# The last batch of a cross-attention kernel: two sets of four PSUM banks in turn, the keys' third chunk projected inside the batch, and a third head's sum off VectorE

## The chip, the cores and the metric

The kernel runs on one core of one Trainium2 chip. The metric is the device time of one execution in microseconds (us). All data are float32. Before the change, four runs took 459.06, 458.02, 459.40 and 457.72 us: the median is 458.54 us. The profiled execution is the one of 459.06 us; its span, from the first to the last instruction on the core, is 457.3 us.

Names used below: PE is TensorE, DVE is VectorE, ACT is ScalarE, POOL is GpSimd, SP is SyncE, on whose queue nearly all DMAs are issued. L617 is line 617 of the kernel. PSUM, where PE writes, has eight banks here, each used as a tile of 128 x 512.

## The reference, cut to what matters

Eight batches; 112 query rows of 320 channels, 20 heads of 16 channels; 371 text rows and 4 prompt rows of 512 channels for each batch.

```python
q, k_t, v_t = heads(x @ W_q), heads(text @ W_k), heads(text @ W_v)
probs_t = softmax(q @ k_t.T * 16 ** -0.5)            # per head: 112 x 371
text_out = probs_t @ v_t
attn_scores = q @ heads(ip @ W_k_ip).T * 16 ** -0.5   # per head: 112 x 4
qsem = l2norm(probs_t @ text)                         # per head: 112 x 512
sem = qsem @ l2norm(ip).T
probs_ip = softmax(attn_scores + 0.5 * sem) * spatial_mask
ip_out = probs_ip @ heads(ip @ W_v_ip)
out = (text_out + ip_out) @ W_out + b_out + x
```

## The kernel before

**Groups.** The 20 heads of a batch are worked on in five groups of four (`groups`, L70): groups 0 and 1 take heads of the first 128 channels, 2 and 3 those of the second 128, group 4 those of the last 64 channels (the third chunk). The norm of `qsem` needs, for each head, p G p' with G the Gram matrix of the text rows; only its diagonal is needed. So for each head PE multiplies the transposed probabilities with a tile `u`, which holds the upper triangle of G with its diagonal halved, the products with the normalised prompts, a column of ones and the values of the head (`multiplied`, L603). That gives 392 columns for each head in one PSUM bank (`ps_qd`): the first 371 are summed against `p`, and the last 21 are copied out as `pvs`. The four heads of a group lie in four row strips of the array and run side by side; a group is 12 rounds j of four matmuls that get 32 columns narrower from round to round, each in two passes.

**The stages of a group**, each two groups ahead of the next: `scores` on PE (112 x 371 into a bank of its own); `probabilities`, which is the row maximum `nmx` on DVE (L582), the exponential `p` on ACT (L586) and a DMA of `p` into `xg` on SP's queue (L589); `transposed`, one large transpose `xgT` on DVE (L597); then `multiplied` on PE; then the copy of `pvs` (L630) on ACT and the sum `junk`, `ss` on DVE (`reduced`, L657). With LEAD = 2, the scores of group g+2 are issued among the rounds of group g, and DVE does the transpose of group g+1 right behind the four `nmx` of group g+2.

**Order.** PE, SP and DVE run in the order in which the code is written; ACT too in the main loop, and POOL too in the last batch. `p` has three buffers for each head group (L584, `bufs=3`), so that the exponential of group g+3 writes where `p` of group g was.

**The last batch** (b = 7, from L999) has no next batch whose projections could fill PE's waits. Four steps differ there. In groups 0 to 2 (`g <= LEAD`) the first two heads' sums are taken off DVE (`shared`, L632): ACT copies the product out of PSUM (L642), POOL multiplies it with `p` (L646), and ACT sums it (L650). The banks are chosen by hand: `ps_qd` has four banks, `ps_sc` (`bank(..., spare=True)`) two and `ps_mm` (`bank(...)`) two. The prompts' part of batch 6 is finished with a block-diagonal matrix `bd`: `own_channels` (L519) cuts `bd` out with a memset and two selections on POOL. And `finish` (L670) is stepped by hand: its parts stand between the groups' work on DVE, ACT, POOL and PE.

**The end of a batch**, `finish`: `z`, `rn` (DVE, from `pvs` and `ss`), square root (ACT, L704, which needs a load of its function table, and another one back to the exponential, L705), `zr` (L707) and `attn` (POOL, L710), `rn`, `fu`, `mx`, `fu` (DVE, L715 to L721), `ex` (ACT, L725), `sx`, `rx`, `w` (DVE, L729 to L733); then with `bd` the transpose `ps_wT` (PE, L739) and its copy (ACT, L743), the matmuls `ps_a` (PE, L749 and L752), their copy `aT` (ACT, L760), the output projection `ps_o` (PE, L767) and `ob` (DVE, L780), which goes out by DMA (L783). For batch 6 this runs among groups 2 to 4 of batch 7 and behind them. Batch 7 is finished in two parts: `first` (heads 0 to 15, with `bd`) and `last` (heads 16 to 19, without it).

**Two more helpers.** `keys` (L433) projects the keys in three chunks; for all batches but the first, the third chunk's 64 channels come out of `values` (L460), whose matmuls are 384 columns wide instead of 320, and are copied by POOL (L476) and transposed by PE (L441). `prompt_logits` (L542) multiplies the queries with the prompts' keys (`ps_ip`, three small matmuls) and copies the result on ACT (`ipl`, L556).

Of the kernel before, what the change touches and what calls it, by code (L numbers as in the profile page):

```python
# [8 lines left out]
F32 = mybir.dt.float32  # L9
AF = mybir.ActivationFunctionType  # L10
ALU = mybir.AluOpType
# [9 lines left out]
def kernel(  # L21
# [343 lines left out]

    def awake(n, end=False):

        if end:
            ps = ps_qd.tile([P, 512], F32, tag="qd", name=f"ps_w_{n}")
        else:  # L370
            ps = bank(f"ps_w_{n}", spare=True)
        for _ in range(n):
            nc.tensor.matmul(ps[:, :P], ident, ident, start=True, stop=True)  # L373

# [58 lines left out]
    def keys(b):  # L433
        s = st[b]
        for i in range(NC):
            ps = bank(f"ps_k_{b}_{i}")
            if b > 0 and i == FULL:

                for c in range(NT):
                    rows = min(P, TT - c * P)  # L440
                    nc.tensor.transpose(  # L441
                        ps[:, c * P : c * P + rows],
                        s["k3"][:rows, c].rearrange("p a r d -> p (a r d)"),
                        ident[:rows, :rows],
                    )
                nc.scalar.copy(s["kT"][:, i, :], ps[:, :TT])
                yield
                return
            for e in range(NE):
                nc.tensor.matmul(  # L450
                    ps[:, :TT],
                    wk_sb[:, e, i * P : (i + 1) * P],
                    s["ctxT"][:, e, :TT],
                    start=(e == 0),
                    stop=(e == NE - 1),
                )
            nc.scalar.copy(s["kT"][:, i, :], ps[:, :TT])  # L457
            yield

    def values(b):  # L460
        s = st[b]
        ctxT, vext = s["ctxT"], s["vext"]
        w = C + REST if b > 0 else C
        for c in range(NT):
            ps = bank(f"ps_v_{b}_{c}")
            for e in range(NE):
                nc.tensor.matmul(  # L467
                    ps[:, :w],
                    ctxT[:, e, c * P : (c + 1) * P],
                    wv_sb[:, e, :w],  # L470
                    start=(e == 0),
                    stop=(e == NE - 1),
                )
            nc.scalar.copy(vext[:, c, :w], ps[:, :w])  # L474
            if w > C and c == NT - 1:
                nc.gpsimd.tensor_copy(  # L476
                    s["k3"][:, :, :, 0, :],
                    vext[:, :, C:].rearrange("p c (a d) -> p c a d", d=D),
                )
            yield  # L480
# [122 lines left out]
    def multiplied(b, g):  # L603
        s = st[b]
        xT = s.pop(("xT", g))
        banks = []
        for a in range(GROUP):


            if b == B - 1 and (g, a // 2) in ((1, 0), (2, 1), (3, 1), (4, 1)):  # L610
                banks.append(bank(f"ps_qd_{b}_{g}_{a}", spare=g == 3))
            else:
                banks.append(ps_qd.tile([P, 512], F32, tag="qd", name=f"ps_qd_{b}_{g}_{a}"))
        for j in range(BLK):
            c, q = j // QN, j % QN
            for a in range(GROUP):
                nc.tensor.matmul(  # L617
                    banks[a][:S, j * RG : UW],
                    xT[a * RG : (a + 1) * RG, j, :S],
                    region(b, c)[a * RG : (a + 1) * RG, q, q * RG :],  # L620
                    start=(j == 0),
                    stop=(j == BLK - 1),
                )
            yield
        s["qd", g] = banks
# [6 lines left out]
    def shared(b, g):  # L632

        s = st[b]
        some = list(enumerate(zip(groups[g], s["qd", g])))[:2]
        t = work.tile([P, NE, TP], F32, tag="ctxT", name=f"shared_{b}_{g}")
        prods = [t[:S, a, :TT] for a, _ in some]
        p = s["p", g]
        for a, (h, ps) in some:
            if b == B - 1:  # L640
                nc.scalar.copy(s["pvs"][:, h, :], ps[:S, TT:UW])
            nc.scalar.copy(prods[a], ps[:S, :TT])  # L642
        yield

        for a, _ in some:
            nc.gpsimd.tensor_tensor(prods[a], prods[a], p[:, a, :], ALU.mult)  # L646
        yield

        for a, (h, _) in some:
            nc.scalar.activation(prods[a], prods[a], AF.Copy, accum_out=s["ss"][:, h : h + 1])  # L650
        yield
# [18 lines left out]
    def finish(b, heads=(0, H), eng=None, late=False, bd=None):  # L670
# [18 lines left out]
        if not late:  # L689
# [14 lines left out]
        nc.scalar.activation(rn, rn, AF.Sqrt)  # L704
        nc.scalar.preload_act_table(AF.Exp)  # L705
        zr = sm("zr")
        nc.vector.reciprocal(zr, z)  # L707
        attn = attn_ring[b % 2]
        ah = attn[:, :C].rearrange("p (h d) -> p h d", d=D)[:, part]
        eng.tensor_tensor(  # L710
            ah, pvs[:, :, NIP + 1 :], zr.unsqueeze(2).to_broadcast([S, n, D]), ALU.mult
        )
        yield

        nc.vector.reciprocal(rn, rn)  # L715
        fu = sm4("fu")
        nc.vector.tensor_tensor(fu, pvs[:, :, :NIP], over_ip(rn), ALU.mult)
# [13 lines left out]
        nc.vector.reciprocal(rx, sx)  # L731
        w = sm4("w")
        nc.vector.scalar_tensor_tensor(w, ex, sm_sb, over_ip(rx), ALU.mult, ALU.mult)  # L733
        yield

        i0, i1 = h0 * D // P, -(-h1 * D // P)
        if bd is not None:
            ps = ps_qd.tile([P, 512], F32, tag="qd", name=f"ps_wT_{b}")
            nc.tensor.transpose(  # L739
                ps[: n * NIP, :S], w.rearrange("s h n -> s (h n)"), ident[:S, :S]  # L740
            )
# [45 lines left out]
    def prompt_sums_and_projection(b, s, eng, part, n, h0, h1, i0, i1, w, attn, ah, late):  # L787
# [14 lines left out]
            eng.tensor_tensor(ah, ah, wv[:, 1], ALU.add)  # L802
        yield

        ps = bank(f"ps_a_{b}_{h0}", spare=True)
        for i in range(i0, i1):
            nc.tensor.transpose(
                ps[:, i * S : (i + 1) * S], attn[:, i * P : (i + 1) * P], ident[:S, :S]
# [34 lines left out]
    def between(b, g):  # L843
# [26 lines left out]
        if g == 3:  # L870
            if new:
                run(("k", nb), None, 1)
            for bs in first if b > 0 else ():
                run(("q", bs[0]), lambda: project_queries(bs), 3)
            if new:
                run(("t", b), lambda: prompt_logits(b))
            if new:
                run(("k", nb), None, 1)
            if b > 0 and new:
                run(("f", b - 1), None)  # L880
            for bs in rest:
                run(("q", bs[0]), None)
        if g == 4:
            if nb + 1 < B:
                run(("c", nb + 1), lambda: transposed_context(nb + 1))
            if b > 0 and new:
                run(("f", b - 1), None, 2)
            if nb + 1 < B:
                run(("c", nb + 1), None, 2)
            for bs in (first if b > 0 else []) + rest:  # L890
                run(("q", bs[0]), None)
            if nb == B - 1:
                run(("t", nb), lambda: prompt_logits(nb))

    prompts = normalised_prompts()
    context = transposed_context(0)
# [103 lines left out]
    b = B - 1  # L1000
    before = ("f", b - 1)

    places = {0: {0: (2, 3), 1: (0, 1)}, 1: {0: (2, 3), 2: (0, 1)}, 2: {0: (2, 3), 2: (0, 1)}}
    for g in range(NG):
        own = {}
        for a in (0, 1) if g in places else ():
            if g == 0:
                own[a] = bank(f"ps_s_{b}_{g + LEAD}_{a}")
            elif g == 2:
                own[a] = ps_qd.tile([P, 512], F32, tag="qd", name=f"ps_s_{b}_{g + LEAD}_{a}")  # L1010
        for j, _ in enumerate(multiplied(b, g)):
            for a in places.get(g, {}).get(j, ()):
                if g == 1 and a < 2:
                    own[a] = ps_qd.tile([P, 512], F32, tag="qd", name=f"ps_s_{b}_{g + LEAD}_{a}")
                scores(b, g + LEAD, a, ps=own.get(a))
                probabilities(b, g + LEAD, a)
            if j != 2:
                continue
            drain(sums)
            if g == 2:  # L1020
                run(before, lambda: finish(b - 1, bd=bd[:, 0]))
            if g + 1 < NG:
                transposed(b, g + 1)
            if g == 3:
                run(before, None, 2)
                nc.scalar.preload_act_table(AF.Sqrt)  # L1026
        if g <= LEAD:
            sums = shared(b, g)
            next(sums)
            value_sums(b, g, 2)  # L1030
            reduced(b, g, 2)
        else:
            value_sums(b, g)
            if g == NG - 1:
                run(before, None)
                next(first)
                run(before, None)
                nc.scalar.preload_act_table(AF.Sqrt)
                run(before, None)
            reduced(b, g)  # L1040
        if g + 1 < NG:
            placed(b, g + 1)
        if g <= LEAD:
            next(sums)
        if g == 0:
            run(("f", b - 2), None)
        if g == 1:
            prompt_values(b)
            own_channels(bd)
        if g == 2:  # L1050
            run(before, None)
        if g == 3:

            first = finish(b, (0, FULL * HC), bd=bd[:, 1])
            next(first)
            next(first)
            run(before, None)
            next(first)
# [58 lines left out]
```

## Time and profile before

| what | us |
|---|---|
| median of four runs | 458.54 (457.72 to 459.40) |
| the profiled run, and its span | 459.06, 457.3 |
| busy in the span: PE, DVE, ACT, POOL | 437.8, 308.8, 191.0, 107.8 |
| busy in the last 17 us: PE, DVE, ACT, POOL | 11.14, 6.08, 4.17, 0.00 |
| one transpose `xgT` (L597), one `nmx`, one `p`, one `junk` | 2.97, 0.53, 0.57, 0.54 |
| one POOL product of `shared` (L646), one selection on `bd` (L524) | 0.97, 1.00 |

A busy PE is not PE at its peak, since matmuls are pipelined. The chain of waits follows the work that ended last back from the last instruction; in this execution it goes back to 410.92 us, into the last batch. In a timeline row the numbers are start and length in us, then engine, line, operation, tiles and count, and in brackets how long the engine was idle before it and whom it waited for. In a table of stretches, each row gives the stretch, its length, and busy time (and instructions) of PE, of PE's weight loads, DVE, ACT and POOL, then PE's granted clock as a share of full speed, the share of DMA and its GB/s.

### The profile page before, as it was taken

What the parts mean: (1) busy time and instruction counts of PE and PEld (TensorE: products, weight loads), DVE (VectorE), ACT (ScalarE), POOL (GpSimd) and SP (SyncE); (2) the same over time, 40 slices, a digit from 0 to 9 for tenths busy, and PEclk for the clock granted to TensorE, in tenths of its full rate; (3) what the DMA queues carried; (4) which work ended last, traced back from release to release, by engine and by line L of the source; (5) the groups of instructions that cost most, each with busy time, mean ns of one, the idle gap of its engine ahead of it and who ended that gap; (6) DMA issues with size and microseconds to landing.
All of it is one profiled execution on the core that took longest, in us unless ns stands there. A gap on an engine that the chain in (4) does not pass through costs nothing. (4 is left out here: it accounts for less than half of the span.)

```text
span 457.3 us, 12952 instructions
## 1 busy us (share of the span) xinstructions
PE 437.8 (96%) x5132; PEld 340.0 (74%) x5132; DVE 308.8 (68%) x657; ACT 191.0 (42%) x531; POOL 107.8 (24%) x260
## 2 busy tenths in 40 slices
PE   8998999999999999999999999999999999988855
PEld 8756867877777877887778877887768777878743
DVE  3047466786677768786676668787677668778763
ACT  2254233345334353345334353345335353355631
POOL 4302200102051114212061113312050213336400
PEclk9999999999999999999999999999999999999967
DMA  8569954645646454645646554545655355535200
GB/s 251 154 172 258 200 158 109 148 129 162 160 127 163 141 135 137 146 131 165 170 115 155 156 147 130 138 139 154 170 139 137 118 131 157 140 88 156 58 0 25
DMA packets 52158, 64.83 MB, mean 142 GB/s; under 512 B 18370, under 2 KB 44146, under 8 KB 52098
## 3 DMA queue, kind: packets, MB, share of 16 engines
q1 hardware_dynamic: 51658, 63.45, 52.2%
q8 instruction: 40, 0.66, 0.6%
q10 hardware_dynamic: 440, 0.56, 0.4%
q14 instruction: 20, 0.16, 0.1%
HBM read 19.30 MB, written 5.32 MB: 54 GB/s over the span
## 5 line engine op out<-in xcount | busy, mean ns | idle before, releaser
L617 PE MATMUL ps_qd<-u,xgT 32*112 32x104 f32 (+11 forms) x3840 | 216.6, 351 | 5.5 <-DVE xgT L597 3.2
L617 PEld LDWEIGHTS ps_qd<-u,xgT 32*112 32x112 f32 x3840 | 183.8, 172 | 39.1 <-issue 9.1
L582 DVE TENSOR_REDUCE nmx<-ps_s 112x1 f32<-112x371 f32 x160 | 77.6, 529 | 75.0 <-PE ps_s L569 74.3
L597 DVE STREAM_TRANSPOSE xgT<-xg 128x1536 f32<-128x1536 f32 x40 | 118.9, 2972 | 7.5 <-DMA xg<-p 7.5
L586 ACT ACTIVATE p<-ps_s,nmx 112x371 f32<-112x371 f32 x160 | 82.5, 572 | 64.3 <-DVE nmx L582 52.3
L657 DVE CUSTOM_DVE_ANT_0 junk<-ps_qd,p 112x371 f32<-112x371 f32 x152 | 82.4, 542 | 18.1 <-ACT pvs L630 2.0
L538 POOL COPY u<-vr 128x64 f32<-128x64 f32 x120 | 26.2, 240 | 173.6 <-PE ps_qd L617 117.7
L467 PE MATMUL ps_v<-wv_sb,ctxT 128*128 128x384 f32 (+1 forms) x192 | 64.7, 487 | 0.0
L569 PE MATMUL ps_s<-kT,qm 32*112 32x371 f32 x320 | 63.8, 475 | 0.4 <-ACT p L586 0.4
L467 PEld LDWEIGHTS ps_v<-wv_sb,ctxT 128*128 128x128 f32 x192 | 35.2, 190 | 20.8
L450 PE MATMUL ps_k<-ctxT,wk_sb 128*128 128x371 f32 x136 | 45.9, 482 | 0.0
L630 ACT COPY pvs<-ps_qd 112x21 f32<-112x21 f32 x154 | 16.1, 190 | 64.9 <-PE ps_qd L617 64.8
L414 PE MATMUL ps_g<-ctxT 128*128 128x375 f32 (+2 forms) x168 | 37.4, 379 | 0.0
L450 PEld LDWEIGHTS ps_k<-ctxT,wk_sb 128*128 128x128 f32 x136 | 25.1, 190 | 15.4 <-issue 0.5
L414 PEld LDWEIGHTS ps_g<-ctxT 128*128 128x128 f32 x168 | 28.1, 190 | 8.4
L569 PEld LDWEIGHTS ps_s<-kT,qm 32*112 32x112 f32 x320 | 26.1, 171 | 4.8 <-ACT kT L457 2.1
L312 DVE TENSOR_SCALAR qm<-ps_q,emask 128x224 f32<-128x224 f32 (+1 forms) x25 | 9.2, 400 | 26.2 <-PE ps_q L303 26.1
L474 ACT COPY vext<-ps_v 128x384 f32<-128x384 f32 (+1 forms) x24 | 11.3, 472 | 27.2 <-PE ps_v L467 26.6
L457 ACT COPY kT<-ps_k 128x371 f32<-128x371 f32 x17 | 8.0, 469 | 26.8 <-PE ps_k L450 26.8
L402 ACT ACTIVATE ug<-ps_g 128x375 f32<-128x375 f32 (+2 forms) x24 | 9.0, 377 | 23.0 <-PE ps_g L414 19.8
L403 POOL TENSOR_TENSOR ug<-ug,half 128x128 f32<-128x128 f32 (+1 forms) x24 | 10.8, 452 | 29.6 <-ACT ug L402 29.6
L789 POOL TENSOR_TENSOR wv<-vip,w 112x1280 f32<-112x1280 f32 x6 | 14.8, 2462 | 11.3 <-DVE w L733 11.3
(123 smaller groups left out, 331.2 us busy)
## 6 DMA issues: line engine op xcount, KB each, us to landing
xg<-p SPq DMA_DIRECT2D x160, 162.3 KB
u<-ug SPq DMA_DIRECT2D x128, 99.0 KB
ct<-in_ctx_dram SPq DMA_DIRECT2D x16, 256.0 KB
vip<-vipd SPq DMA_DIRECT2D x7, 560.0 KB
vr<-vd SPq DMA_DIRECT2D x32, 120.0 KB
vd<-vext SPq DMA_DIRECT2D x7, 320.0 KB
ct<-in_ctx_dram SPq DMA_DIRECT2D x8, 224.0 KB
vd<-vext SPq DMA_DIRECT2D x7, 160.0 KB
```

What stands on the lines that cost most here:

```text
L414: nc.tensor.matmul(ps[:, : T - t0], ctxT[:, e, t0 : t0 + P], ctxT[:, e, t0:T], start=(e == 0), stop=(e == NE - 1),)
L450: nc.tensor.matmul(ps[:, :TT], wk_sb[:, e, i * P : (i + 1) * P], s["ctxT"][:, e, :TT], start=(e == 0), stop=(e == NE - 1),)
L467: nc.tensor.matmul(ps[:, :w], ctxT[:, e, c * P : (c + 1) * P], wv_sb[:, e, :w], start=(e == 0), stop=(e == NE - 1),)
L538: nc.gpsimd.tensor_copy(region(b, c)[:, :, UV - c * P :], s["vr"][:, c * QN : (c + 1) * QN, g, :])
L569: nc.tensor.matmul(ps[:S, :TT], qm[a * RG : (a + 1) * RG, i, r, j * S : (j + 1) * S], s["kT"][a * RG : (a + 1) * RG, i, :], start=True, st ...
L582: nc.vector.tensor_reduce(nmx, ps[:S, :TT], AX.X, ALU.max, negate=True)
L586: nc.scalar.activation(p, ps[:S, :TT], AF.Exp, bias=nmx)
L597: nc.vector.transpose(xT.rearrange("p j (k q) -> p q j k", q=QN), xg.rearrange("p q (j k) -> p q j k", k=RG),)
L617: nc.tensor.matmul(banks[a][:S, j * RG : UW], xT[a * RG : (a + 1) * RG, j, :S], region(b, c)[a * RG : (a + 1) * RG, q, q * RG :], start=(j ...
L630: nc.scalar.copy(s["pvs"][:, h, :], ps[:S, TT:UW])
L657: nc.vector.tensor_tensor_reduce(out=junk, in0=ps[:S, :TT], in1=s["p", g][:, a, :], scale=1.0, scalar=0.0, op0=ALU.mult, op1=ALU.add, accu ...
L789: eng.tensor_tensor(wv, s["vip"][:, :, part], w.rearrange("p h n -> p n h").unsqueeze(3).to_broadcast([S, NIP, n, D]), ALU.mult,)
```

## The change

For the last batch alone:

- Odd groups (1 and 3) multiply into `ps_mm` and `ps_sc`, even groups into `ps_qd`. The scores of group 2 go to `ps_mm` and `ps_sc`, those of group 3 to `ps_qd`, those of group 4 to `ps_mm` and `ps_sc` again; their places and the order of the heads change (`coming`).
- The third chunk of the keys is projected by itself (`last_keys`, four matmuls), in two halves behind group 0, with the scores of two heads of group 3 between the halves. `values` of batch 7 is 320 columns wide, and the POOL copy and the transposes of the third chunk are gone.
- `prompt_logits` of batch 7 moves from the end of batch 6 to behind group 0.
- `shared` takes three heads of a group instead of two. At the end of batch 6 it still takes two, in another buffer.
- `own_channels` moves from behind group 1 to behind group 3.
- In `finish` with `bd`, `zr` stands one step later and POOL's `attn` three steps later. The banks of `ps_wT`, of the warm-up matmuls `ps_w` and of the last `ps_a` change.

```diff
     def awake(n, end=False):
-        if end:
-            ps = ps_qd.tile([P, 512], F32, tag="qd", name=f"ps_w_{n}")
-        else:
-            ps = bank(f"ps_w_{n}", spare=True)
+        ps = bank(f"ps_w_{n}", spare=not end)
...
-            if b > 0 and i == FULL:
+            if 0 < b < B - 1 and i == FULL:
...
+    def last_keys(b, ps):
+        s = st[b]
+        for e in range(NE):
+            if e == NE // 2:
+                yield
+            nc.tensor.matmul(
+                ps[:, :TT],
+                wk_sb[:, e, FULL * P :],
+                s["ctxT"][:, e, :TT],
+                start=(e == 0),
+                stop=(e == NE - 1),
+            )
+        nc.scalar.copy(s["kT"][:, FULL, :], ps[:, :TT])
+        yield
...
-        w = C + REST if b > 0 else C
+        w = C + REST if 0 < b < B - 1 else C
...
-            if b == B - 1 and (g, a // 2) in ((1, 0), (2, 1), (3, 1), (4, 1)):
-                banks.append(bank(f"ps_qd_{b}_{g}_{a}", spare=g == 3))
+            if b == B - 1 and g % 2 and g < NG - 1:
+                banks.append(bank(f"ps_qd_{b}_{g}_{a}", spare=a > 1))
...
-        some = list(enumerate(zip(groups[g], s["qd", g])))[:2]
+        some = list(enumerate(zip(groups[g], s["qd", g])))
+        if b == B - 1:
+            some = some[: GROUP - 1]
...
-        nc.vector.reciprocal(zr, z)
...
+        if bd is None:
+            nc.vector.reciprocal(zr, z)
+            divided()
+        yield
+        if bd is not None:
+            nc.vector.reciprocal(zr, z)
         nc.vector.reciprocal(rn, rn)
...
         nc.vector.scalar_tensor_tensor(w, ex, sm_sb, over_ip(rx), ALU.mult, ALU.mult)
+        if bd is not None:
+            divided()
...
-            ps = ps_qd.tile([P, 512], F32, tag="qd", name=f"ps_wT_{b}")
+            ps = bank(f"ps_wT_{b}")
...
-        ps = bank(f"ps_a_{b}_{h0}", spare=True)
+        ps = bank(f"ps_a_{b}_{h0}", spare=not late)
...
-            if nb == B - 1:
-                run(("t", nb), lambda: prompt_logits(nb))
...
-    places = {0: {0: (2, 3), 1: (0, 1)}, 1: {0: (2, 3), 2: (0, 1)}, 2: {0: (2, 3), 2: (0, 1)}}
+    def coming(g, heads):
+        for a in heads:
+            if g == 1:
+                ps = ps_qd.tile([P, 512], F32, tag="qd", name=f"ps_s_{b}_{g + LEAD}_{a}")
+            else:
+                ps = bank(f"ps_s_{b}_{g + LEAD}_{a}", spare=a > 1)
+            scores(b, g + LEAD, a, ps=ps)
+            probabilities(b, g + LEAD, a)
     for g in range(NG):
...
+        if g == 1:
+            keys3 = last_keys(b, ps_qd.tile([P, 512], F32, tag="qd", name=f"ps_k_{b}_{FULL}"))
+            next(keys3)
+            coming(g, (3, 0))
+            next(keys3)
+        places = {0: {0: (2, 3), 1: (0, 1)}, 1: {0: (1, 2)}, 2: {1: (3, 0), 2: (1, 2)}}.get(g, {})
         for j, _ in enumerate(multiplied(b, g)):
+            coming(g, places.get(j, ()))
...
-            value_sums(b, g, 2)
-            reduced(b, g, 2)
+            value_sums(b, g, GROUP - 1)
+            reduced(b, g, GROUP - 1)
...
         if g == 0:
+            drain(prompt_logits(b))
             run(("f", b - 2), None)
         if g == 1:
             prompt_values(b)
-            own_channels(bd)
         if g == 2:
             run(before, None)
         if g == 3:
+            own_channels(bd)
```

## The prediction

> **What bounds the kernel now.** I read the page first: its slices show where PE stops being full and where its clock falls.
>
> ```profile
> span 457.3 us, 12952 instructions
> ...
> PE   8998999999999999999999999999999999988855
> PEclk9999999999999999999999999999999999999967
> ```
>
> Up to some 405 us PE is full, so there every saved matmul is saved time; from the 36th slice on something else decides. Second, a table of stretches, one row for each group of the last batch (start of its first matmul to start of the next group's):
>
> ```profile
> 411.38:418.40 7.02, 5.62 (x104) 5.54 (x105) 6.13 (x10) 4.20 (x15) 3.05 (x6) 1.00 0.52 149
> 418.40:425.82 7.42, 5.63 (x105) 5.54 (x105) 6.19 (x12) 4.87 (x15) 5.91 (x11) 1.00 0.64 177
> 425.82:430.70 4.88, 4.86 (x97) 4.21 (x97) 4.14 (x8) 3.15 (x7) 1.84 (x4) 1.00 0.10 30
> ```
>
> Groups 1 and 2 take 7.02 and 7.42, of which PE works 5.6: the loop is scores, four `nmx`, `xgT`, next group. Group 3 needs 4.88. Third, the chain of waits and timeline rows from its later part:
>
> ```profile
> 424.06 3.33 DMA xg<-p
> ...
> 427.51 2.98 DVE xgT L597
> ...
> 431.47 0.54 DVE fu L721
> ...
> 432.31 1.28 ACT L1026
> ...
> 433.82 0.55 DVE junk L657
> ...
> 440.91 0.77 PE ps_a L749 x2
> ...
> 444.35 3.54 PE ps_o L767 x6
> ...
> 451.85 1.98 DMA out_dram<-ob
> ```
>
> The end hangs on group 4's probabilities landing (427.39), `xgT`, batch 6's `fu`, a table load, `pvs`, `junk`; then on `ps_a`, which starts only at 440.91:
>
> ```profile
> 440.91 0.77 PE L749 MATMUL ps_a<-ident,attn 112*128 112x112 f32 x2 [2.58 <-DVE ss L657]
> ...
> 438.61 0.27 ACT L743 COPY wT<-ps_wT 80x112 f32<-80x112 f32 x1
> ...
> 431.03 0.86 POOL L695 TENSOR_TENSOR xb<-x_sb,bias_sb 112x320 f32<-112x320 f32 x1
> ...
> 431.47 0.52 DVE L721 TENSOR_TENSOR fu<-fu,mx 112x80 f32<-112x80 f32 x1
> ...
> 419.53 2.08 POOL L524 TENSOR_SCALAR_AFFINE_SELECT bd<-bd 80x640 f32<-80x640 f32 x2
> ```
>
> `wT` was ready at 438.88; `ps_a` waited for a bank of group 4 that the third `junk` still read. And `fu` took 0.52 instead of 0.24 beside POOL's `xb`: it ended 0.1 behind it.
>
> **The change, part by part** (times on the profile's own scale).
>
> Before group 0. Twelve `ps_v` matmuls shrink from 384 to 320 columns: eight passes took 2.68 at 384 (380.53 to 383.21) and, in batch 0, 2.165 at 320 (16 passes from 16.37 to 20.70). Three chunks save 3 x 0.515 = 1.55, by width alone (a sixth of 2.68) 1.34; I take 1.45. The three transposes of `k` go: 0.34 (394.57 to 394.91) up to 0.49 with the gap ahead of them; 0.40. `ps_ip` leaves 403.84 to 404.86: 1.02. Together 2.87. Nothing else holds PE there: group 0's `xgT` was ready 3.4 ahead of its use, POOL's columns of `u` 4.3. Group 0 starts at 402.0 and ends, 5.42 later as before, at 407.4.
>
> Between groups 0 and 1 a block is added on PE: `ps_ip` (six passes, 0.65 by the row at 393.75), half the keys (four passes at 2.59/8: 1.30), two scores side by side (two passes each, 0.65), the other half (1.30): 3.9. Behind it PE queues group 1. Its own waits, for ACT's copies of three banks (ready at 407.98, 408.4 and 408.85, by 0.43 each), end before their turn. Group 1 starts at 411.3, against 411.38: the block eats the 2.87 and the 1.10 that PE waited there for ACT's copies (now another set of banks, so that wait is gone).
>
> Group 1. Only two scores are left behind round 0, so `nmx` ends not at the second pair (+3.98) but at +2.65 (413.04 + 0.99, against 411.38): 413.95. `xgT` and 0.14 more put group 2 at 417.05, against 418.40. DVE's dropped `junk` (0.70) is no part of this: it stood ahead of a wait for scores (0.39 idle).
>
> Three heads off DVE. ACT gets one copy (0.43) and one sum (0.49) more a group, POOL one product (0.955). ACT has room: it idled 2.2 to 2.7 in each group. POOL has a follower: `p` of group 4 writes where `p` of group 1 was, so it waits for POOL's third product. Bank 0 of group 1 is done 5.51 - 0.28 (two scores fewer at 0.14) behind its start, at 416.55; the copy adds 0.55, three products 2.87: 419.97, and `p` starts at 420.05; its `nmx` is ready at 419.75. Before it started at 420.70: 0.65 gained. SP then issues four DMAs 0.92 apart, which hides the later of the `p`, and the last lands 0.65 earlier, at 426.74; group 4's `xgT` ends at 429.8. Group 3's `xgT` gains more than that: in group 2 the second pair of scores now stands behind pair and round 2, ready some 3.5 behind the start instead of 2.99, so group 3 starts at 424.85 (gain 0.97) and ends at 429.75. The next in line is still the landing.
>
> `zr` moves onto the way from `xgT` to `fu`: +0.20. Then `fu`'s chain ends at 431.5 if nothing holds it (before 432.0).
>
> `own_channels` moves on POOL from 419.4, beside `nmx`, to behind group 3's last copy of `u` (430.1): memset, two selections of 1.04, `xb` 0.87, `attn` 0.74, until 433.95. Exactly there DVE does three operations with two SBUF operands (L717, L718, L721). The row of `fu` shows such an operation held to the end of POOL's; so do `rn` at 155.88 (0.33 instead of 0.18, beside `ug` 155.70 to 156.17) and `w` at 437.38 (0.43 instead of 0.30, beside `attn`). `junk`, with one operand in PSUM, took 0.55 beside POOL's products, as ever. A selection beside a two-operand operation is not in this trace. Bounds: 0, as beside `junk`, `fu` at 431.5; or each of the three held in turn, `fu` at 433.3. The `fu` row is nearest in kind; I take two and a half of three, 432.9.
>
> [...]
>
> The end. From `fu` to the copy of `wT` were 6.88 (432.00 to 438.88: table load, `pvs`, four `junk`, square root, table load, `pvs`); the removed `zr` shortens only `w`, which has room. So 439.8. `ps_a` now takes a bank that group 3 gave back: its first pair (0.57) is done before `wT`, and it no longer waits 2.03 for DVE. Five pairs of 0.43 and 0.2 to the copy: `aT` at 442.2 against 443.86. Sum: 2.03 + 0.57 - 0.9 - 0.05 = **1.65** gained; all behind it (`ps_o`, `ps_w`, `wT`, `ex`, `ob`, its DMA) slides along.
>
> At nothing: other bank of `ps_w`; `shared` of batch 6 in another buffer (POOL left it 10 earlier); `kT` and `ipl` copies (0.70 on ACT, hidden under `p`'s wait until 410.97; if `p` did not wait they would cost it up to 0.2); later `attn` (done 433.95, used 438.6); SP's count of DMAs, which is the same.
>
> Span 457.3 - 1.65 = 455.65. The profiled run, 459.06, lies 0.52 above the median of the runs, so the median goes from 458.54 to **456.9**.
>
> **Rivals.**
>
> *The hold does not happen:* POOL's selections pass beside DVE. For it: transposes and `junk` ran beside POOL unharmed. Against: three rows of held operations. `fu` 431.5, gain 3.05: 455.5. Chance 0.22.
>
> *The block stays uncovered (slower):* PE's saving before group 0 does not arrive, since DMAs, ACT or DVE hold group 0 where it was, and the block pushes all that follows. Against: PE shows no waits from 385 to 403. For: the chain of waits says nothing before 410.92. Each lost us costs one: with none of the 2.87 the time is 458.54 + 1.2 = 459.8; slower from 1.65 lost on. Chance 0.15.
>
> *PE stays cold longer:* its clock was 0.50 from 437.95 to 448.15, ten us after an idle of 2.4. The new idle (434.7 to 438.6) will drop it too. If it stays low through the last six `ps_o` passes (0.53 instead of 0.29 each) and the `ps_a` ahead of them, some 1.4 are lost: 458.3. For: work starts 1.65 earlier, the clock perhaps not. Against: `ps_o` and `ps_w` run 4.4 without a gap, as before. Chance 0.13.
>
> *The change does nothing there:* no; as built, `ps_a` waits for POOL's `attn` and ACT's copies only, not for `junk`.
>
> **How the numbers follow.** Forecast 0.50, rivals 0.22, 0.15 and 0.13. I call 0.3% (1.38) what a measurement can tell: faster means below 457.16. The forecast (spread about 0.9, from the holds and the landing) puts 0.60 of itself there, the first rival nearly all: 0.30 + 0.21 + 0.03 from the others = 0.54, to which early clocks add little: 0.56. Slower is under half of the uncovered block and a tail of the cold clock: 0.12. Same: 0.32. The range reaches down beyond the unheld case, 455.0, and up to the uncovered block, 459.6.
>
> **What would show it.** Right: group 0 starts near 402, group 1 near 411.3, group 2 near 417; `p` of group 4 waits for POOL `shared`; `fu` rows beside `bd` last up to 1 us; `ps_a` follows `wT` directly, `aT` some 1.7 earlier. Wrong: group 1 starting after 413, `fu` unheld, or a clock that comes back after the last `ps_o`.

## The result, and the profile after

The changed kernel takes 457.22 us (median of 53 runs, 453.10 to 460.15), the kernel before 458.02 (median of 79 runs); the ratio is 0.997 with a 95% interval of 0.9961 to 0.998. That is faster by 0.92 to 1.79 us; the difference of the medians is 0.80. Two executions of the changed kernel, both 460.15 us, count as slow and are left out of the ratio. The forecast was 456.9, with a range of 455.0 to 459.6.

The page of the profiled execution (457.91 us), its span and two of its rows of slices:

```profile
span 456.2 us, 12979 instructions
...
PE   8998999999999999999999999999999999999765
...
PEclk9999999999999999999999999999999999999967
```

PE's dip begins two slices later than before, at the 38th instead of the 36th: the last batch is fuller. But the clock's row is the same as before, and those last two slices hold the low clock that the rest of this document turns on.

The table of stretches for the last batch: the block between groups 0 and 1, then groups 1, 2 and 3, each from its first matmul to the next group's:

```profile
406.92:411.31 4.39, 4.39 (x23) 2.29 (x19) 2.62 (x5) 2.37 (x10) 2.94 (x4) 1.00 0.50 143
411.31:416.95 5.64, 5.42 (x102) 4.80 (x101) 3.92 (x3) 3.50 (x12) 0.49 (x3) 1.00 0.39 107
416.95:424.46 7.51, 5.48 (x105) 4.80 (x105) 5.69 (x9) 5.67 (x22) 4.92 (x9) 1.00 0.48 145
424.46:429.99 5.53, 4.80 (x96) 4.15 (x97) 3.67 (x5) 4.76 (x11) 3.18 (x8) 1.00 0.16 47
```

Group 1 takes 5.64 instead of 7.02, and PE works in nearly all of it. Group 2 still takes 7.5, and the block costs 4.39.

Timeline rows of the steps that the prediction named:

```profile
420.00 1.96 ACT L599 ACTIVATE p<-ps_s,nmx 112x371 f32<-112x371 f32 x4 [1.84 <-POOL shared L666]
...
429.81 2.09 POOL L537 TENSOR_SCALAR_AFFINE_SELECT bd<-bd 80x640 f32<-80x640 f32 x2
...
430.08 0.79 DVE L744 TENSOR_TENSOR fu<-pvs,rn 112x80 f32<-112x80 f32 x1
430.91 1.04 DVE L745 SCALAR_TENSOR_TENSOR fu<-fu,ipl 112x80 f32<-112x80 f32 x1
...
431.87 0.86 POOL L715 TENSOR_TENSOR xb<-x_sb,bias_sb 112x320 f32<-112x320 f32 x1
...
432.26 0.57 DVE L748 TENSOR_TENSOR fu<-fu,mx 112x80 f32<-112x80 f32 x1
...
438.80 0.69 PE L778 MATMUL ps_a<-ident,attn 112*128 112x112 f32 x2
...
439.45 0.27 ACT L772 COPY wT<-ps_wT 80x112 f32<-80x112 f32 x1
...
439.77 0.77 PE L781 MATMUL ps_a<-wT,bd 80*128 80x112 f32 x2 [0.28 <-ACT wT L772]
```

`p` of group 4 now waits for POOL's product, not for its maximum; three operations of `fu` last two to four times as long as without company (0.24), the first two beside the selections, the third beside `xb`, which POOL starts behind them; and `ps_a` follows `wT` at once, where it waited 2.03 for `junk` before.

The chain of waits shows what the end then hangs on:

```profile
417.26 2.71 POOL shared L666 x3
...
420.00 1.96 ACT p L599 x4
...
423.37 3.38 DMA xg<-p
...
442.77 3.54 PE ps_o L796 x6
446.31 1.28 PE ps_w L370 x6
```

`ps_o` starts 1.58 earlier than before (444.35), but `ps_w` behind it ends only 1.17 earlier, and the last `ob` starts 1.14 earlier.

**One mark for all executions.** Profiled executions differ by up to 1.3 us ahead of anything that was edited: the first matmul of `values` for batch 7 starts at 369.82 before, at 369.50 in the changed kernel, and between 368.54 and 369.76 in the experiments. So from here on times in "from the mark" are counted from that matmul, and compared with the kernel before in the same count. The table has the end of `fu` of batch 6, the start of its `aT`, and the start of the last `ob`; the last column adds up, over the rows of the granted clock by single microseconds from 415 us to 450 us, twice what each lacks to 1.00, which gives the time spent at half clock (in bank_fill all of it lies behind the start of the last `ob`, in p4_ob2 the second low clock goes on past 450).

| kernel | `fu` ends | `aT` starts | last `ob` starts | against before | at half clock, us |
|---|---|---|---|---|---|
| before | 62.17 | 74.04 | 84.13 | | 10.24 |
| changed | 63.33 | 72.78 | 83.31 | -0.82 | 10.24 |
| bank_only | 62.24 | 71.68 | 81.28 | -2.85 | 6.82 |
| own_back | 62.00 | 71.46 | 81.11 | -3.02 | 6.82 |
| keys_back | 62.63 | 72.08 | 82.67 | -1.46 | 10.24 |
| warm | 63.34 | 72.01 | 80.46 | -3.67 | 0 |
| p4_ob2 | 61.28 | 69.64 | 82.87 | -1.26 | 15.30 |
| four | 61.75 | 71.20 | 81.53 | -2.60 | 10.24 |
| bank_warm | 61.78 | 71.37 | 79.64 | -4.49 | 3.40 |
| four_warm | 60.62 | 70.29 | 78.23 | -5.90 | 3.42 |
| after_fill | 63.40 | 71.74 | 80.52 | -3.61 | 0 |
| four_fill | 62.27 | 70.62 | 78.58 | -5.55 | 0 |
| four_fill5 | 61.76 | 70.11 | 79.65 | -4.48 | 3.42 |
| bank_fill | 62.38 | 70.72 | 79.24 | -4.89 | 1.08 |

Counted so, the changed kernel gains 0.82 in its profile, which is what the medians say (0.80). Each row is one execution, and the runs of a kernel differ by more than some of these steps, so the ratios below stand beside them.

### The profile page after: what moved, and what is told of

Same layout as the page of the kernel before. It is cut to its first block, busy times and chain, and to the rows that moved or that the text cites. A ratio compares the mean times of both kernels' runs of the same rounds, so it can differ in the third digit from the quotient of the medians.

```text
span 456.2 us, 12979 instructions
## 1 busy us (share of the span) xinstructions
PE 439.5 (96%) x5137; PEld 339.9 (75%) x5137; DVE 309.9 (68%) x651; ACT 193.0 (42%) x540; POOL 109.5 (24%) x262
## 4 chain that ended last, share of the span: by engine, by line
PE 91%; ACT 3%; DVE 3%; DMA 1%; POOL 1%; issue 1%; DVEq 0%; POOLq 0%; ACTq 0%
PE ps_qd L629 40%; PE ps_v L480 14%; PE ps_k L447 10%; PE ps_g L411 8%; PE ps_s L582 4%; PE ps_q L303 3%; PE ps_c L353 2%; PE ps_o L849 2%; PE ps_g L383 1%; DMA xg<-p 1%; PE ps_w L370 1%; PE ps_o L796 1%; PE ps_ip L562 1%; ACT p L599 1%; DVE xgT L610 1%; PE ps_k L463 1%
## 5 line engine op out<-in xcount | busy, mean ns | idle before, releaser
L677 DVE CUSTOM_DVE_ANT_0 junk<-ps_qd,p 112x371 f32<-112x371 f32 x149 | 80.9, 543 | 20.1 <-ACT pvs L642 4.4
L480 PE MATMUL ps_v<-wv_sb,ctxT 128*128 128x384 f32 (+1 forms) x192 | 63.5, 480 | 0.0
```

Source lines behind the costliest of these rows:

```text
L480: nc.tensor.matmul(ps[:, :w], ctxT[:, e, c * P : (c + 1) * P], wv_sb[:, e, :w], start=(e == 0), stop=(e == NE - 1),)
L677: nc.vector.tensor_tensor_reduce(out=junk, in0=ps[:S, :TT], in1=s["p", g][:, a, :], scale=1.0, scalar=0.0, op0=ALU.mult, op1=ALU.add, accu ...
```

## The experiments

Each ratio is to the kernel before, with its 95% interval, and each comes from runs on one chip. The runs of the kernel before beside them had medians of 458.00 (first four experiments), 457.47 (next four) and 458.10 (last four).

**bank_only: of the whole change, only the bank of `ps_a`, made in the kernel before.**

```diff
-            ps = bank(f"ps_a_{b}_{h0}")
+            ps = bank(f"ps_a_{b}_{h0}", spare=b < B - 1)
```

> The kernel before, with one edit: the tile ps_a of batch 6 is taken from ps_sc instead of ps_mm, so that it no longer needs a bank that the third junk of group 4 still reads. Theory (the freed bank alone is what the change gained): the first pair of ps_a is done before wT is there (438.88), the copy aT starts at about 441.4 instead of 443.86, ps_o at 441.9 instead of 444.35; part of these 2.4 is given back by a clock still at 0.50 under ps_w, as in the changed kernel (1.58 there became 1.14), and the run is some 1.5 us faster than the kernel before, ratio about 0.9967, level with or ahead of the changed kernel. Rival (the earlier groups of the last batch brought part of the gain): clearly less than the changed kernel, under 0.6 us.

Measured: 455.84 us, ratio 0.9939 (0.9916 to 0.9962). Timeline rows of its end:

```profile
438.07 0.63 PE L749 MATMUL ps_a<-ident,attn 112*128 112x112 f32 x2
...
438.56 0.27 ACT L743 COPY wT<-ps_wT 80x112 f32<-80x112 f32 x1
...
441.39 0.44 ACT L760 COPY aT<-ps_a 128x336 f32<-128x336 f32 x1 [2.09 <-PE ps_a L752]
```

`aT` starts at 441.39, as expected (441.4). One argument in one line gains 2.85 from the mark where the whole change gains 0.82: in these profiles the rest of the change costs about 2.0. By the ratios it is less, 0.61% against 0.30%, or some 1.4 us, and the two intervals touch. The time gained was more than the 1.5 expected; in the profile the clock helped. In a table of stretches (the last number but two is the granted clock), the low clock of bank_only and what follows it:

```profile
437.90:444.70 6.80, 6.10 (x19) 4.45 (x20) 5.13 (x25) 4.39 (x11) 0.00 (x0) 0.50 0.00 0
444.70:451.48 6.78, 4.91 (x24) 3.08 (x22) 2.72 (x8) 0.96 (x4) 0.00 (x0) 1.00 0.07 21
```

and that of the changed kernel:

```profile
438.62:447.30 8.68, 7.87 (x25) 6.00 (x26) 5.55 (x26) 4.55 (x11) 0.71 (x1) 0.50 0.00 0
447.30:453.30 6.00, 4.30 (x18) 2.27 (x16) 2.71 (x8) 0.96 (x4) 0.00 (x0) 0.98 0.08 24
```

bank_only has its full clock back under `ps_w`, after 6.82 us, the changed kernel after 10.24. Of the difference at the last `ob` (2.03), 1.10 was there at `aT`; the other 0.93 came between `aT` and `ob`, with the longer low clock.

**own_back: the changed kernel with `own_channels` back in its old place.**

```diff
         if g == 1:
             prompt_values(b)
+            own_channels(bd)
...
         if g == 3:
-            own_channels(bd)
```

> The changed kernel, with own_channels back behind group 1. Theory (POOL's selections hold DVE's operations on two SBUF operands): the three operations of fu last 0.22 to 0.25 each instead of 0.79, 1.04 and 0.57, fu ends near 431.2 instead of 432.83, wT's copy ends near 438.0 instead of 439.72, and the run is 1.2 to 1.7 us faster than the changed kernel (ratio to the kernel before about 0.994). z and rn of batch 6 would then stand beside the selections and last up to 1 us longer, which delays group 3 by as much, without reaching the end. Rival (no hold, they are slower for another reason): the fu rows stay at 0.6 to 1.0 each and the time is that of the changed kernel.

Measured: 455.64 us, ratio 0.9922 (0.9895 to 0.995). Timeline rows beside the selections and of `fu`:

```profile
420.30 2.09 POOL L537 TENSOR_SCALAR_AFFINE_SELECT bd<-bd 80x640 f32<-80x640 f32 x2
...
421.41 0.97 DVE L721 TENSOR_TENSOR rn<-ss,z 112x20 f32<-112x20 f32 x1
...
430.39 0.24 DVE L744 TENSOR_TENSOR fu<-pvs,rn 112x80 f32<-112x80 f32 x1
430.67 0.24 DVE L745 SCALAR_TENSOR_TENSOR fu<-fu,ipl 112x80 f32<-112x80 f32 x1
430.69 0.96 POOL L715 TENSOR_TENSOR xb<-x_sb,bias_sb 112x320 f32<-112x320 f32 x1
...
431.21 0.53 DVE L748 TENSOR_TENSOR fu<-fu,mx 112x80 f32<-112x80 f32 x1
```

The hold moved with the selections: `rn`, 0.18 in the changed kernel, lasts 0.97 and ends at 422.38, 0.01 before they do; the first two operations of `fu` are back at 0.24. The third is held by `xb`, as before the change. `fu` ends 1.33 earlier from the mark. The gain at the last `ob`, 2.2 against the changed kernel, is again 1.3 at `aT` and 0.9 more with a low clock of 6.82 instead of 10.24. The rival is out: the rows went back to 0.24, and the interval lies below the changed kernel's.

**keys_back: the changed kernel with the third chunk of the keys out of `values` again.**

```diff
-            if 0 < b < B - 1 and i == FULL:
+            if b > 0 and i == FULL:
...
-        w = C + REST if 0 < b < B - 1 else C
+        w = C + REST if b > 0 else C
...
-            if nb < B - 1:
+            if new:
                 run(("k", nb), None, 1)
...
-            keys3 = last_keys(b, ...)
-            next(keys3)
             coming(g, (3, 0))
-            next(keys3)
```

> The changed kernel, with the third chunk of the keys out of values again (384 columns, the copy on POOL and three transposes before group 0), and without the four matmuls behind group 0; the two scores and ps_ip stay there. Theory (the block behind group 0 costs PE 2.9, the old way 1.85, and nothing idles now that could pay for it): group 0 starts at about 403.5 instead of 401.6, but group 1 at 410.4 instead of 411.35, and all that follows is 0.8 to 1.0 earlier, so the run is 0.6 to 0.9 us faster than the changed kernel. Rival (the block fills a time in which group 1 would wait anyway, for ACT's and POOL's work on group 0): group 1 starts no earlier than 411.2 and the run is level or up to 1 us slower.

Measured: 456.15 us, ratio 0.9953 (0.9935 to 0.997). The block in the timeline:

```profile
408.59 0.76 PE L562 MATMUL ps_ip<-kipb,qT 128*112 128x32 f32 x6
409.28 1.32 PE L582 MATMUL ps_s<-kT,qm 32*112 32x371 f32 x4
410.38 1.18 PE L629 MATMUL ps_qd<-u,xgT 32*112 32x392 f32 x9
```

Group 0 starts 1.89 later from the mark than in the changed kernel, group 1 0.71 earlier (expected 0.95), and at `xgT` of group 4, `fu` and `aT` it is still 0.7. The last `ob` is 0.64 earlier. The third chunk thus costs more behind group 0 (2.89, two halves of 1.45) than in its old place, and nothing there pays for it. The rows show this; the ratio's interval overlaps the changed kernel's, so the runs alone do not.

**warm: the changed kernel with twelve warm-up matmuls behind group 4; they compute nothing that is used.**

```diff
+        if g == NG - 1:
+            awake(12)
         if g <= LEAD:
             sums = shared(b, g)
```

> The changed kernel, with twelve more warm-up matmuls on PE right behind group 4's last one, into a free bank; they compute nothing that is used. Theory (PE's idle of 3.6 us behind group 4 drops its clock to 0.50 for some 10 us, and this clock sets the end): the granted clock stays at 1.00 from 435 to 449, the pairs of ps_a take 0.25 instead of 0.43, ps_o 1.8 instead of 3.54, and the end is 2.5 to 3.4 us earlier than in the changed kernel (ratio to the kernel before about 0.990). Rival (the end hangs on ACT's and DVE's chain of heads 0 to 15, PE waits for it anyway): ps_o ends early and the gain is under 1 us.

Measured: 456.27 us, ratio 0.9942 (0.9919 to 0.9965). A timeline row, and the stretch in which the changed kernel had half clock:

```profile
436.29 2.94 PE L370 MATMUL ps_w<-ident 128*128 128x128 f32 x24 [1.61 <-DVE ss L677]
```

```profile
438.62:447.30 8.68, 7.50 (x43) 5.59 (x42) 7.20 (x31) 5.11 (x14) 0.52 (x1) 1.00 0.01 2
```

In the profiled execution the theory holds: the clock stays full, `ps_o` takes 1.87 instead of 3.54, the last `ob` comes 2.85 earlier than in the changed kernel. Over the runs the gain is smaller: six of the eight had a mean clock of 0.994 to 0.996, so they did lose some time at half clock. The gain over the changed kernel is some 1.3 us by the ratios, between the theory (2.5 to 3.4) and the rival (under 1). The profile can't show where the low clock was, since it had none; the next runs could.

**p4_ob2: the changed kernel with memory of its own for `p` of group 4 and for the last `ob`.**

```diff
-            s["p", g] = work.tile([S, GROUP, TT], F32, tag="p", ..., bufs=3)
+            if (b, g) == (B - 1, NG - 1):
+                t = io.tile([P, NT, E], F32, tag="ct", ...).rearrange("p c e -> p (c e)")
+                s["p", g] = t[:S, : GROUP * TT].rearrange("p (a t) -> p a t", t=TT)
+            else:
+                s["p", g] = work.tile([S, GROUP, TT], F32, tag="p", ..., bufs=3)
...
-        ob = work.tile([S, C], F32, tag="ob", ..., bufs=1)
+        if b == B - 1:
+            ob = work.tile([P, NT, C + REST], F32, tag="vext", ..., bufs=1)[:S, 0, :C]
+        else:
+            ob = work.tile([S, C], F32, tag="ob", ..., bufs=1)
```

> The changed kernel, with memory of its own for p of group 4 (the context tile that nothing reads any more) and for the last ob (the values' tile). A look at rows, since 0.6 us is less than single executions differ by. Theory (POOL's third product of group 1 holds p of group 4): the first p of group 4 waits for its nmx alone and starts 0.3 after where the third product would have let it, counted from group 2's first matmul: 2.75 instead of 3.05; the last xg lands and xgT starts 0.3 earlier against the same mark. The last ob starts within 0.1 of its ps_o instead of 0.37 behind it, where it waited for the DMA of the ob before. Rival (SP's queue of DMAs sets the landing): p starts earlier, the landing does not.

Measured: 456.64 us, a single run. Timeline rows of `p` of group 4 and of the last `ob`, and, in stretches, PE's group 3:

```profile
418.82 1.96 ACT L603 ACTIVATE p<-ps_s,nmx 112x371 f32<-112x371 f32 x4 [1.55 <-DVE nmx L595]
...
451.48 0.49 DVE L816 TENSOR_TENSOR ob<-ps_o,xb 112x320 f32<-112x320 f32 x1 [4.77 <-PE ps_o L856]
```

```profile
424.27:427.70 3.43, 3.43 (x32) 2.53 (x28) 2.05 (x1) 3.39 (x8) 1.20 (x2) 0.53 0.07 22
427.70:434.66 6.96, 6.96 (x160) 6.25 (x156) 4.53 (x18) 2.36 (x8) 4.37 (x8) 0.99 0.01 2
```

Both waits are gone: `p` waits for its maximum and starts 2.77 behind group 2's first matmul (3.05 in the changed kernel), `xgT` of group 4 starts 9.60 behind it instead of 9.92, and `ob` waits for PE. The landing came earlier with `p`, so the rival of SP's queue is out. What nobody had in mind is the second fence: the clock fell to half in group 3, for 3.41 us, from 424.46 on, 0.9 behind the end of an idle time of 2.05 on PE. Here a low clock followed a wait of group 3, as one followed group 4's wait of 3.59 in the changed kernel's profile. That is one place where single executions of one kernel part. A second low clock, from 438.1 on, lasted past 450 us here, so that this execution's last `ob` is only 1.26 ahead of the kernel before although its `aT` is 4.40 ahead.

**bank_warm, four, four_warm.** bank_warm is bank_only with `awake(10, end=True)` in the place of warm's edit. four joins the edits of keys_back and p4_ob2 in the changed kernel, with `own_channels` behind group 0. four_warm is four with `awake(13, end=True)`.

> bank_only with ten more warm-up matmuls on PE right behind group 4, into a bank of ps_qd that group 3 has given back by then (in the run warm the bank came free only 1.6 us after PE went idle). Theory (the clock's low windows are the next limit): the granted clock stays at 1.00 to the end in the profile, aT comes at 440.3 instead of 441.39, ex of the last four heads at 443.5 instead of 446.13, and the run is 2 to 2.6 us faster than bank_only, ratio to the kernel before 0.988. Rival (low windows come whatever PE does, as the single runs of warm at a mean clock of 0.996 suggest): under 1 us faster than bank_only, ratio 0.992 or more.

> The changed kernel with four edits: own_channels behind group 0, the third chunk of the keys out of values again, and memory of their own for p of group 4 and for the last ob. Theory (the four losses are independent and add up: 1.2 to 1.6 from the held operations, 0.9 from the keys, 0.3 from p, 0.35 from ob): fu ends near 430.2, w near 435.8, and the run is 2.7 to 3.2 us faster than the changed kernel, ratio to the kernel before 0.989. Rival (the clock's windows of 3.4 us swallow part of it, since the end then falls wholly into them): about the time of own_back, 0.992.

> The run four with thirteen warm-up matmuls behind group 4, into a bank that the first junk of group 3 gives back. Theory: no low clock at the end, the last ob near 446.5, ratio to the kernel before 0.985, ahead of bank_warm by what the groups gain. Rival (with PE fast, the chain of DVE and ACT for the last four heads is what ends last, the same in both): level with bank_warm.

Measured: 453.51 us, ratio 0.9918 (0.99 to 0.9935); 455.09 us, 0.9948 (0.9931 to 0.9965); 453.67 us, 0.9905 (0.9883 to 0.9927). In bank_warm and four_warm the clock is full from 429 us to past the start of the last `ob`, though both show a low one of 3.4 us in group 3, and the warm-up matmuls ran too long: `ps_wT` came 1.8 and 2.0 behind `w`. Both missed their theories (0.988 and 0.985) and came out at their rivals: bank_warm is 1.0 us ahead of bank_only by the ratios, and four_warm is level with bank_warm. That the chain for the last four heads made them level, as the second rival has it, was not tried. four is a miss too, 1.0 us ahead of the changed kernel where 2.7 to 3.2 were expected. In its timeline and its stretches:

```profile
428.07 0.87 POOL L719 TENSOR_TENSOR xb<-x_sb,bias_sb 112x320 f32<-112x320 f32 x1
428.90 0.74 POOL L735 TENSOR_TENSOR attn<-pvs,zr 112x320 f32<-112x320 f32 x1
...
428.17 0.87 DVE L748 TENSOR_TENSOR fu<-pvs,rn 112x80 f32<-112x80 f32 x1
429.08 0.67 DVE L749 SCALAR_TENSOR_TENSOR fu<-fu,ipl 112x80 f32<-112x80 f32 x1
```

```profile
435.61:445.85 10.24, 8.96 (x29) 6.68 (x30) 6.10 (x28) 5.38 (x13) 0.71 (x1) 0.52 0.00 0
```

With the selections away, POOL's `xb` and `attn` moved up into their place and held `fu` instead, by 1.06 (0.87 and 0.67 against 0.24 each). From the mark, `fu` is 1.58 earlier than in the changed kernel, not 2.6, and a low clock of 10.24 instead of own_back's 6.82 left the last `ob` 0.42 behind own_back's although `aT` was 0.26 ahead. Both halves of "add up" failed.

**after_fill, four_fill, four_fill5, bank_fill: warm-up matmuls in PE's idle times.** after_fill is the changed kernel with

```diff
     for g in range(NG):
+        if g == 3:
+            awake(6, end=True)
...
+        if g == NG - 1:
+            awake(12, end=True)
         if g <= LEAD:
```

four_fill is four with the same and 10 at the end, four_fill5 with 5; bank_fill is bank_only with `awake(5)` before groups 2 and 3 and 8 at the end.

> The changed kernel with PE's two longest idle times filled with warm-up matmuls: six before group 3 (idle 2.03, they take 1.5) and twelve behind group 4 (idle 3.59, they take 2.9). Theory (a stretch with PE idle for some 2 us sets off a low window of the clock, whether it does depends on where a grid of 3.4 us falls in the execution, and these windows are the spread and a good part of the end): the granted clock is 1.00 from 400 us on, single executions lie closer together than the 7 us of the changed kernel, and the ratio to the kernel before is 0.990. Rival (the windows come anyway): 0.994 or more, with windows in the profile.

> The run four, filled in the same way: six warm-up matmuls before group 3, ten behind group 4. Theory (without the clock's windows the four edits keep their whole worth, 1.2 to 1.6 + 0.9 + 0.3 + 0.35): 2.5 to 3.1 us faster than after_fill, ratio to the kernel before 0.984. Rival (the last four heads' chain on DVE and ACT takes over): under 1.5 us faster than after_fill.

> As four_fill, with five instead of ten behind group 4. It tells how long an idle time the clock bears. Theory: PE then idles some 1.7 us before ps_wT, a low window comes in part of the executions, and the median is up to 1.5 us slower than four_fill. If no window comes: level with four_fill or up to 0.3 us faster, where ten held ps_wT up.

> bank_only (the kernel before with another bank for ps_a) with warm-up matmuls in its idle times: five before group 2 (idle 1.39) and group 3 (1.79), eight behind group 4 (idle 2.4; the ten of bank_warm held ps_wT up by 1.8). Theory: no low window, ps_wT right behind w, ratio to the kernel before 0.987, and four_fill is 1 to 1.5 us ahead of it by its earlier groups and its own memory for ob. Rival: level with bank_warm, 0.992.

| kernel | us | ratio, 95% interval | single runs |
|---|---|---|---|
| after_fill | 454.45 | 0.9924 (0.991 to 0.9938) | 454.19 to 455.32 |
| four_fill | 453.12 | 0.9896 (0.9875 to 0.9918) | 452.18 to 455.37 |
| four_fill5 | 453.65 | 0.9899 (0.9885 to 0.9913) | 453.01 to 453.80 |
| bank_fill | 453.71 | 0.9907 (0.989 to 0.9923) | 452.99 to 455.08 |

The stretches of after_fill, from group 3 to the last `ob`:

```profile
424.00:434.06 10.06, 9.25 (x192) 8.02 (x184) 6.51 (x10) 6.34 (x15) 6.16 (x11) 1.00 0.08 21
434.06:437.82 3.76, 2.94 (x24) 2.78 (x25) 3.14 (x15) 0.97 (x2) 0.00 (x0) 1.00 0.00 0
437.82:449.64 11.82, 8.52 (x41) 5.64 (x41) 8.17 (x34) 5.61 (x15) 0.71 (x1) 1.00 0.05 14
```

No half clock is left there, and the runs lie within 1.13 us of each other (three of the five with a mean clock of 1.00, two with 0.997). So in these profiles the idle times make the low clock, and filling them takes it away. The ratio of 0.9924 lies between the theory (0.990) and the rival (0.994 or more). four_fill5, with 1.46 idle ahead of `ps_wT`, shows one low stretch of 3.41 from 439.5 on as expected, yet it is level with four_fill in its ratio. Two expectations failed. four_fill is 1.3 ahead of after_fill, not 2.5 to 3.1, which is the rival's number: `xb` held `fu`, and the last landing of `p` took 4.40 where it took 3.36 in four. Where this came from was not tried. And bank_fill is level with four_fill: their intervals cover each other. It is also level with bank_warm (0.9918), as its rival said. All four beat both the kernel before and the changed one.

## Why the prediction was right

Its time and range held, and most of its steps did; from the mark:

| step | forecast against before | measured |
|---|---|---|
| group 0 starts earlier by | 2.87 | 2.97 |
| the block | 3.9 long | 4.39 long |
| group 1 starts | -0.08 | +0.25 |
| group 2 starts | -1.35 | -1.13 |
| `p` of group 4 starts | -0.65 | -0.38 |
| group 3 starts | -0.97 | -1.04 |
| `xgT` of group 4 starts | -0.65 | -0.32 |
| `fu` ends | +0.9 | +1.16 |
| `aT` starts | -1.65 | -1.26 |
| last `ob` starts | -1.65 | -0.82 |

*Before group 0 and the block.* The saving arrived whole, which ends the rival of the uncovered block as it was put. The block was mis-sized by 0.5: the halves of the keys took 1.44 each, not 1.30, and the two scores 0.82, not 0.65; PE was busy all through it. Group 1 started 0.33 later than forecast by that, and group 2, `p` and `xgT` of group 4 came 0.2 to 0.3 later too.

*POOL's third product* holds `p`, as reckoned: `p` starts 0.03 behind it, and 0.29 earlier from the mark without it (p4_ob2).

*The hold* of DVE by POOL's selections was the step chosen between two ends, two and a half of three. All three operations were held: 0.79, 1.04 and 0.57 against 0.24, together 1.68, the third by `xb`. The rival "the hold does not happen" is out; own_back shows it, where the first two go back to 0.24. The forecast put 1.4 on top of 431.5, and that base was not free of holds: 432.0 - 0.65 + 0.20 still has in it the 0.28 by which `xb` held the old `fu`. So 1.68 was right for the hold in all, and the 0.26 by which `fu` came later than forecast goes back to the 0.33 of `xgT`. The second of the three ends at 431.95, the selections at 431.90, and the reduction `mx`, with one operand in SBUF and beside `xb`, takes 0.24. With all three held in turn, the upper of its two bounds, the prediction had put `fu` at 433.3; on the scale of the kernel before (mark plus 63.33) it ended at 433.15.

*`ps_a`* no longer waits for `junk`. bank_only shows that this term, 2.03 + 0.57 = 2.60, is more than the whole gain: alone it moves `aT` by 2.36.

*"All behind it slides along"* is the step that failed. Between `aT` and the last `ob` the changed kernel gave back 0.44. The rival of the cold clock had the mechanism right and the place wrong: it reckoned with the last six passes of `ps_o`, for batch 7, which ran at full clock in both profiles (1.33 for four, 0.79 for two); the six of batch 6 were at half clock in both (3.54). The loss is in `ps_w` and `ps_wT` ahead of them, which before ran mostly at full clock and now did not: `ps_w` took 1.28 in the chain instead of 0.87. In p4_ob2's execution the last six were cold too, 2.48 and 1.41. What I did not see at all is how near the end lay to a whole step of the clock: bank_only, 1.1 us earlier at `aT`, has one low stretch of three less and gains 0.9 more. An earlier start alone does not do it: four is 1.6 earlier and kept all three. The mean clocks of the runs say that it also differs between executions: 10.24 us at half clock alone bring the mean over 456 us down to 0.989, and of the kernel before none of the 38 runs beside the experiments is above that; 18 of 53 of the changed kernel are (0.990 and 0.992), 5 of 6 of bank_only and of own_back, none of 6 of four.

The forecast gain was 1.65; from the mark the profile has 0.82, the medians 0.80, the ratio over all runs 1.37 (0.92 to 1.79). The mechanism was right and its size too large, by the block and by the clock.

## What to carry to other kernels

Take a large change apart before you keep it: here the one line that freed a bank was worth more than the whole, twice as much by the ratios (0.61% against 0.30%) and more than three times in the profiles (2.85 against 0.82), and the rest of it cost time, by a block in a stretch that had lost its idle time and by POOL's work put beside DVE's operations on two SBUF operands (0.79 and 1.04 instead of 0.24). Moving such POOL work away helps only if nothing else of POOL moves up into its place, as `xb` and `attn` did in four, where they held `fu` by 1.06. At an end where PE is idle for 2 us and more (2.39 before, 3.59 in the changed kernel, each followed by a granted clock of 0.50), look at that clock first: a few matmuls that compute nothing, fitted to the idle time and into a bank that is free, took the changed kernel's ratio from 0.997 to 0.9924, some 2 us more, which is more than its own gain.

## What the runs showed of the hardware

The half clock comes in whole steps: added up over the profiles it is 3.40 to 3.42 (bank_warm, four_warm, four_fill5, group 3 of p4_ob2), 6.82 (bank_only, own_back) and 10.24 us (before, changed, keys_back, four), so one, two and three steps of 3.41. A low step followed an idle time on PE ahead of group 3 of 2.05 in p4_ob2, 2.03 in four_warm and 1.79 in bank_warm, and none followed the 2.03 of the changed kernel's profile or the 1.79 of the kernel before.

The clock's records in the traces tell why. In the traces of the kernel before and of the changed kernel every change of the clock lies a whole number of steps of 3.413 us behind the first one (before: 7.87, then 437.95, 448.19 and 455.02, 126, 129 and 131 steps on; changed: 7.23, then 437.31, 447.55 and 454.37, the same numbers of steps on). Counted back 123 such steps from its low clock at 424.46, the first one of p4_ob2 would be at 4.62. PE's first matmul is at 1.44 in the traces of both kernels, so the grid does not start with the kernel. Add up PE's idle time within each step of this grid: in these two traces the four full steps that a low one followed had 1.84 to 2.39 us, the 252 that a full one followed 1.52 or less. In the experiments' rows from 415 to 450 us, with the grid laid out from their low clocks, the full steps ahead of a low one had from 1.47 (four_fill5) to 2.55 (keys_back), so the two ranges overlap by 0.05. The 2.03 of the changed kernel was cut by an edge at 423.65 into 1.23 and 0.81, the 1.79 of the kernel before into 0.27 and 1.52. This was read from the traces afterwards; no run moved an edge on purpose.

When the full clock comes back is less plain. PE idles 0.52 to 0.53 between the last `ps_a` and `ps_o` in these profiles. Where that gap fell at the start of the second low step (within 0.1 of it in bank_only and own_back), the clock was full after it; where it fell further in (2.46 behind its start before, 1.52 in the changed kernel, 1.28 in keys_back, 1.08 in four), a third step followed. That is a pattern in six profiles, and p4_ob2 does not fit it: its second low step (441.53 to 444.94) had no idle time on PE at all, and the clock stayed low. So what brings the full clock back stays open; no run put the gap on one side or the other on purpose.
